# A gated cross-attention block: queries' features turned by VectorE in blocks and SBUF copies, and a reordered cycle

## The chip, the cores and the metric

The kernel runs on one core of a Trainium2 chip. The metric is the device time of one execution in microseconds (us), lower is better; several runs are taken and their median counts. A profile of one execution records every instruction of the five engines: TensorE (PE, matrix products, with its weight loads as PEld), VectorE (DVE), ScalarE (ACT), GpSimd (POOL) and SyncE (SP), which here only issues DMA transfers. Each engine works through its own queue in order; engines wait for one another by semaphores.

## The reference

For each of 32 samples, `x` has 256 tokens of 256 features, and the context has 77 rows of 256. All is float32. Two residual blocks follow one another.

The first is cross attention without a softmax. Tokens and context rows are normalized and projected by the same `w_in` to 8 heads of 128 features (`f_q`, `f_k`; values are the keys' features too):

```
cosine = f_q . f_k / (|f_q| |f_k|)
q_ratio = 2 min(var(f_q), 1) / (var(f_q) + 1)        (k_ratio likewise)
mixed  = cw * cosine + vw * cosine * decorr + ww * q_ratio * k_ratio
x      = x + tanh(g_xattn) * ((mixed @ f_v) @ w_out.T + b_out)
```

The weights `cw, vw, ww` and `decorr` are one number per head, from means and the correlation of all queries' features over all samples. The second block is self attention with 16 heads of 16 and a softmax over 256 keys, then two products each followed by a length normalization, and a GELU:

```
z = softmax(q k / 16) v;  z = norm(z @ Wo);  z = norm(z @ Wff)
x = x + tanh(g_ffn) * gelu(z)
```

## The kernel before, in words

A first part of about 140 us loads weights and inputs, forms the sums over all samples and the per-head weights, and brings samples 0 and 1 on their way. Then one loop (its body is the list `cycle`, L1157) runs over cycle numbers `n`. An entry `(ahead, stage, ...)` runs that stage for sample `n + ahead`, so in one cycle self attention of sample `n`, cross attention of `n + 1`, query and key features of `n + 2`, inputs of `n + 3` and the last products of `n - 1` are interleaved. The list is the order: the wrapper `InOrder` (L22) keeps the instructions of PE, ACT, DVE and POOL in program order. Almost all instructions therefore carry the line of the wrapper, L30, and are told apart by their tiles. DMAs from SP (`nc.sync`) aren't wrapped: their place in SP's queue is chosen by the framework when the kernel is built.

A sample's stages that matter here:

- `norm_inputs`, `transpose_inputs` (L194, L205): normalized tokens `xn`, turned by PE and scaled into `xTc`.
- `query_features(b, t, hh)` (L371): per half of the tokens `t` and of the heads `hh`, two products of 128x512 into PSUM, copied to `fq` by ACT (`hh` 0) or DVE (`hh` 1). `fq` is a tile of 128 tokens x 1024 features.
- `scale_queries(b, t)` (L388): DVE statistics of the 8 heads (`qst`, `qt`), POOL's power for 1/length (`rq`), POOL's product that scales `fq` in place, and the ratio into the padded tile `qrps[t]`.
- `transpose_queries(b, t, hh)` (L403): PE turns four 128x128 blocks of `fq` by a product with the identity `ident` into a PSUM tile; ACT or DVE copies it to `fqT`. Four calls a sample: 16 transposes, two ACT copies, two DVE copies.
- `key_features` (L224) forms context features in tiles `fvx` of 128 rows over sample borders; `measure_keys` (L242) takes their statistics in the cycles in which a tile is complete; `align_keys` (L252) copies a sample's 77 rows by DMA to `fv` and `nr`; `weigh_keys`, `scale_keys` (DVE writes the scaled selection `dk`) and `transpose_keys` (PE, `fvT`) follow, then `key_outputs` (`vw`, keys times `w_out`).
- `query_ratios`, `query_scores(b, pair)` (L341, L352): scores of the queries `fqT` and keys `fvT` into `s`; `attend` (L417): `s` times `vw` added to `x`.
- Self attention: `ff_stats`, `ff_norm` (`xf`), `ff_transpose`, `ff_project`, `ff_values`; then four units `u`, each with `scores` (PE to two PSUM tiles `sc`, DVE's maxima `nm`), `exponents` (ACT, with sums), `scale_values` (DVE, `vz`, values over sums) and `mix_values` (PE, `zp`). A unit with the stages listed after its scores is called a cluster. `ff_out` to `ff_gelu` finish sample `n - 1`, `ff_add` adds and stores it.

PSUM tiles for everything but scores and mixes (`mm_tile`) are three, used in turn; a product waits until the copy out of its tile's last user is done. `fqT`, `s`, `xTc`, `xf` have one buffer, `fq` and `fv` two, `x` eight. The x load of a later sample waits for the store of the sample that held its buffer.

Of the kernel before, what the change touches and what calls it, by code (L numbers as in the profile page):

```python
# [8 lines left out]
F32 = mybir.dt.float32  # L9
AF = mybir.ActivationFunctionType  # L10
ALU = mybir.AluOpType
# [3 lines left out]
P = 128  # L15
H = 8
# [17 lines left out]
def gated_block_kernel(  # L34
# [102 lines left out]
    def mm_tile():  # L137
        return ps.tile([P, 512], F32, tag="mm", name="mm")
# [54 lines left out]

    def norm_inputs(b):  # L194

        xn = pa.tile([P, NT, D], F32, tag="xn", name="xn", bufs=1)
        for t in range(NT):
            i = b * NT + t
            pool.tensor_scalar(
                xn[:, t, :], kept[b]["x"][:, t, :], mv_x[:, i, 0:1], rstd_x[:, i : i + 1],  # L200
                ALU.subtract, ALU.mult,
            )
        kept[b]["xn"] = xn
# [106 lines left out]
    def paired(pt, k, pair, rhs):  # L310

        for c in range(2):
            for i in range(2):
                h = 4 * pair + 2 * c + i
                pe.matmul(
                    pt[MA * i : MA * (i + 1), c * S : (c + 1) * S],
                    lhsT=k["fvT"][:, h, 0:MA], rhs=rhs[:, h, :], start=True, stop=True,
                )

    def key_outputs(b, pair):  # L320


        k = kept[b]
        if "vw" not in k:
            k["vw"] = pa.tile([P, 5, D], F32, tag="vw", name="vw", bufs=2)
        pg = mm_tile()
        if pair < 2:
            paired(pg, k, pair, woutT)
# [12 lines left out]
    def query_ratios(b):  # L341

        k = kept[b]
        k["s"] = pa.tile([P, 5, S], F32, tag="s", name="s", bufs=1)
        k["pr"] = mm_tile()
        for t in range(NT):
            pe.matmul(
                k["pr"][:, t * P : (t + 1) * P], lhsT=qrps[t].rearrange("p h w -> p (h w)"),
                rhs=ident, start=(t == 0), stop=False,
            )  # L350

    def query_scores(b, pair):  # L352

        k = kept[b]
        if pair < 2:
            pg = mm_tile()
            paired(pg, k, pair, k["fqT"])
            out = k["s"][:, 2 * pair : 2 * pair + 2, :].rearrange("p g q -> p (g q)")
            (act.copy if pair == 0 else dve.tensor_copy)(out, pg)
            return  # L360
        pg = k.pop("pr")
        for i in range(2):
            for j in range(4):
                n = MR + 16 * i
                pe.matmul(
                    pg[32 * j : 32 * j + n, 0:S], lhsT=k["fvT"][:, 2 * j + i, MA : MA + n],
                    rhs=k["fqT"][:, 2 * j + i, :], start=False, stop=(i == 1),
                )
        act.copy(k["s"][:, 4, :], pg[:, 0:S])

# [17 lines left out]
    def scale_queries(b, t):  # L388

        k = kept[b]  # L390
        fq = k["fq", t]
        m2, n2, rt = head_stats(lambda h: fq[:, h * P : (h + 1) * P], P, H, "q")
        rq = pa.tile([P, H], F32, tag="rq", name="rq")
        rsqrt_of(rq, n2)
        fq_h = fq.rearrange("p (h d) -> p h d", d=P)
        pool.tensor_tensor(
            fq_h, fq_h, rq.unsqueeze(2).to_broadcast([P, H, P]), ALU.mult
        )
        dve.scalar_tensor_tensor(
            qrps[t][:, :, MR], m2, P - 1.0, rt, ALU.min, ALU.mult  # L400
        )

    def transpose_queries(b, t, hh):  # L403
        k = kept[b]
        if (t, hh) == (0, 0):
            k["fqT"] = pa.tile([P, H, S], F32, tag="fqT", name="fqT", bufs=1)
        pt = mm_tile()
        for i in range(4):
            h = hh * 4 + i
            pe.transpose(  # L410
                pt[:, i * P : (i + 1) * P], k["fq", t][:, h * P : (h + 1) * P], ident
            )
        out = k["fqT"][:, hh * 4 : hh * 4 + 4, t * P : (t + 1) * P]
        src = pt.rearrange("p (h q) -> p h q", q=P)
        (dve.tensor_copy if hh else act.copy)(out, src)

    def attend(b, t):  # L417

# [215 lines left out]
    def load_w_out():  # L634
        nc.sync.dma_start(out=w_out_n, in_=w_out.rearrange("(c p) e -> p c e", p=P))

    wf_n = sw.tile([P, 2, D], F32, name="wf_n")

    def load_ff(*pairs):
        for w_t, w in pairs:  # L640
# [159 lines left out]
        act.copy(w1T.rearrange("p c o -> p (c o)"), pt[:, 0 : 2 * P])  # L800
        act.copy(w2T, pt[:, 2 * P : 2 * P + 3])

    woT = sw.tile([P, 2, D], F32, name="woT")

    def transpose_wo():
        pt = mm_tile()
# [52 lines left out]
    par16 = const.tile([P, 2], F32, name="par16")  # L859
    qrps, vzs = [], []  # L860
    for i in range(2):
        qrps.append(const.tile([P, H, 16], F32, name=f"qrp{i}"))
        vzs.append(const.tile([P, 4, 4, 16], F32, name=f"vz{i}"))
    eyes = const.tile([M, 2, SL], F32, name="eyes")
    offd = sw.tile([P, P], F32, name="offd")
# [3 lines left out]
    def set_constants():  # L869
        dve.memset(sel, 0.0)  # L870
        dve.memset(sel[:, MR + 1 : MR + 2], 1.0)


        pool.memset(par[:, 0:1], 0.0)
        pool.memset(par[:, 1:2], 1.0)
        for j in range(4):
            pool.memset(par[32 * j : 32 * j + 16, 0:1], 1.0)
            pool.memset(par[32 * j : 32 * j + 16, 1:2], 0.0)
        pool.tensor_scalar(par16, par, 1.0 / 16.0, None, ALU.mult)
        for qrp in qrps:  # L880
# [12 lines left out]
        dve.tensor_scalar(offd, ident, -1.0, 1.0, ALU.mult, ALU.add)  # L893
# [64 lines left out]
    for c in range(2):  # L958
        pe.transpose(pt[0:2, c * P : (c + 1) * P], lb[:, c, :], ident)
        pe.transpose(pt[0:2, D + c * P : D + (c + 1) * P], bl[:, c, :], ident)  # L960
    lbT = sw.tile([2, 2 * D], F32, name="lbT")
    dve.tensor_copy(lbT, pt[0:2, :])

    gs = sw.tile([P, 2, D], F32, name="gs")
# [144 lines left out]
    run(0, transpose_queries, 0, 0)  # L1109
    run(0, transpose_queries, 0, 1)  # L1110
    pt = mm_tile()
    pe.matmul(
        pt[:, 0 : 2 * H], lhsT=ones[0:H, :], rhs=dg.rearrange("p w h -> p (w h)"),
# [11 lines left out]
    for pair in (2, 0, 1):  # L1125
        run(0, key_outputs, pair)
    run(1, key_features)
    run(0, transpose_queries, 1, 0)
    run(0, transpose_queries, 1, 1)
    run(0, query_ratios)  # L1130
    for pair in range(3):
        run(0, query_scores, pair)
# [25 lines left out]
        (4, load_queries),  # L1158
        (-1, mix_values, 3),
        (0, scores, 0),  # L1160
        (2, transpose_inputs),
        (0, exponents, 0, 0),
        (-1, ff_out, 0),
        (-1, ff_out, 1),
        (0, exponents, 0, 1),
        (1, transpose_queries, 1, 0),
        (1, transpose_queries, 1, 1),
        (2, query_features, 0, 0),
        (1, query_ratios),
# [48 lines left out]
        (1, ff_project, "q"),  # L1218
# [42 lines left out]
```

## Time and profile before

| what | value |
|---|---|
| median of 3 runs (lowest, highest) | 1499.01 us (1497.58, 1503.09) |
| profiled execution, its own time | 1491.96 us |
| its span, first to last instruction | 1490.2 us |
| PE busy | 1439.0 us, 97% |
| DVE, ACT, POOL busy | 1078.1, 938.0, 531.1 us |
| mean granted TensorE clock | 0.983 |

"Busy" is the time in which an engine works on at least one instruction; products overlap inside PE, so the mean duration of one (273 ns for a transpose) is more than its share of the busy time (66.8 us for 512). A float32 product is recorded as two instructions, a transpose as one. The slices cut the span in 40 equal parts of 37 us and give each engine's busy share in tenths. The chain that ended last follows the waits back from the last instruction. A group line gives line, engine, operation, tiles written and read, shapes and count, then busy us and mean ns, then idle time of the engine ahead of it and what ended it. A window line gives start:end, length, each engine's busy us with counts in the order PE, PEld, DVE, ACT, POOL, then the granted clock, the DMA engines' share and GB/s. A timeline line gives start and duration in us, then the instruction, and in brackets the engine's idle time ahead of it and what ended it; several alike are merged.

### The profile page before, as it was taken

The numbers are of one execution on the slowest core, as the hardware profiler recorded it, in microseconds if no ns is written. First come the engines' busy times: TensorE is split into PE (matmuls) and PEld (weight loads), VectorE is DVE, ScalarE is ACT, GpSimd is POOL, SyncE is SP. The second block draws the span as 40 slices with busy tenths as digits, with TensorE's granted clock in tenths as the row PEclk, the third lists the DMA queues.
The fourth block names the chain that finished last, engine by engine and source line by source line (L and its number), as shares of the span: only waits on it lengthen the run. The fifth ranks groups of instructions, "written<-read, shape, count | busy, mean of one in ns | idle before, by whom it ended". The sixth has DMA issues, their size and how long they took to land.

```text
span 1490.2 us, 26481 instructions
## 1 busy us (share of the span) xinstructions
PE 1439.0 (97%) x9313; PEld 863.3 (58%) x9313; DVE 1078.1 (72%) x3053; ACT 938.0 (63%) x3038; POOL 531.1 (36%) x656
## 2 busy tenths in 40 slices
PE   6898999999999999999999999999999999999985
PEld 5754556666555555666655555665655555655641
DVE  5735678777777777787776777787777768787853
ACT  5621557666667666666667666666666756666675
POOL 5912233433243233333333333333333334333310
PEclk9989999999999999999999999999999999999996
DMA  8500000000000000000000000000000000000000
GB/s 267 169 15 27 9 10 24 21 26 13 21 24 15 24 24 18 29 24 14 19 18 22 24 24 21 27 17 23 17 20 24 19 24 16 18 14 12 8 8 14
DMA packets 26194, 43.31 MB, mean 29 GB/s; under 512 B 6010, under 2 KB 11055, under 8 KB 26062
## 3 DMA queue, kind: packets, MB, share of 16 engines
q1 hardware_dynamic: 25230, 41.63, 8.8%
q8 instruction: 73, 1.20, 0.3%
q14 instruction: 59, 0.48, 0.1%
q10 hardware_dynamic: 832, 0.00, 0.0%
HBM read 22.98 MB, written 8.39 MB: 21 GB/s over the span
## 4 chain that ended last, share of the span: by engine, by line
PE 88%; ACT 3%; DVE 3%; issue 1%; POOL 0%; ACTq 0%; POOLq 0%
PE mm L30 70%; PE sc L30 9%; PE zp L30 8%; ACT e L30 2%; ACT ge L30 1%; DVE u L30 1%; DVE nm L30 1%; ACT L30 0%; DVE kst L30 0%; DVE kt L30 0%; POOL i L30 0%; DVE vz L30 0%; POOL nrx L30 0%; DVE xTc L30 0%; ACT u L30 0%
## 5 line engine op out<-in xcount | busy, mean ns | idle before, releaser
L30 ACT ACTIVATE e<-sc,nm 128x256 f32<-128x256 f32 x1024 | 474.2, 491 | 143.9 <-DVE nm L30 143.9
L30 DVE TENSOR_REDUCE nm<-sc 128x4 f32<-128x1024 f32 x256 | 301.0, 1216 | 115.8 <-PE sc L30 115.8
L30 PE MATMUL mm<-winT,xTc 128*128 128x512 f32 x512 | 243.8, 608 | 6.4 <-DVE xTc L30 2.2
L30 ACT ACTIVATION_READ_ACCUMULATOR e<-sc,nm 128x1 f32 x1024 | 227.8, 222 | 0.0
L30 POOL TENSOR_TENSOR rq<-qt,nhalf 128x8 f32<-128x8 f32 x64 | 105.8, 1654 | 257.1 <-DVE qt L30 257.1
L30 PE MATMUL sc<-q,kTf 32*128 32x512 f32 x1024 | 153.1, 644 | 4.8 <-ACT e L30 4.8
L30 PEld LDWEIGHTS mm<-winT,xTc 128*128 128x128 f32 x512 | 92.2, 190 | 104.3 <-issue 71.4
L30 PE MATMUL mm<-vw,s 128*128 128x256 f32 x640 | 146.9, 384 | 0.0
L30 PE MATMUL zp<-e,vz 128*32 128x256 f32 x2048 | 138.9, 389 | 5.8 <-DVE vz L30 5.8
L30 POOL TENSOR_TENSOR fq<-fq,rq 128x1024 f32<-128x1024 f32 x64 | 135.0, 2109 | 5.0
L30 PEld LDWEIGHTS mm<-vw,s 128*128 128x128 f32 x640 | 119.0, 190 | 28.5 <-issue 13.7
L30 PE MATMUL mm<-w_of,zT 128*128 128x512 f32 x256 | 117.9, 604 | 0.8 <-DVE zT L30 0.8
L30 PEld LDWEIGHTS zp<-e,vz 128*32 128x32 f32 x2048 | 57.4, 110 | 95.5 <-issue 33.3
L30 POOL TENSOR_SCALAR i<-nn 128x2 f32<-128x2 f32 x64 | 14.2, 222 | 274.3 <-ACT ge L30 274.3
L30 ACT COPY vw<-mm 128x512 f32<-128x512 f32 x32 | 18.8, 586 | 145.1 <-PE mm L30 145.1
L30 DVE BATCH_NORM_STATS2 qst<-fq 128x6 f32<-128x128 f32 x512 | 103.9, 276 | 0.0
L30 PE MATMUL mm<-woutT,fvT 128*64 128x256 f32 (+2 forms) x1024 | 100.8, 384 | 0.1
L30 POOL TENSOR_SCALAR rs<-mv 128x1 f32<-128x1 f32 x64 | 15.8, 247 | 237.0 <-DVE mv L30 235.6
L30 PE MATMUL mm<-fqT,fvT 128*64 128x256 f32 (+2 forms) x1024 | 93.9, 383 | 0.0
L30 DVE TENSOR_TENSOR vz<-v,sums 128x128 f32<-128x128 f32 x128 | 86.8, 678 | 4.4
L30 ACT ACT_TABLE_LOAD x64 | 82.1, 1283 | 4.9 <-DMA x<-in_x_dram 4.1
L30 POOL TENSOR_SCALAR xn<-x,mv_x,rstd_x 128x256 f32<-128x256 f32 x64 | 79.1, 1248 | 10.3 <-issue 10.3
(203 smaller groups left out, 2401.3 us busy)
## 6 DMA issues: line engine op xcount, KB each, us to landing
x<-in_x_dram SPq DMA_DIRECT2D x64, 256.0 KB
out_dram<-x SPq DMA_DIRECT2D x32, 256.0 KB
fv<-fvx SPq DMA_DIRECT2D x13, 308.0 KB
ct<-in_ctx_dram SPq DMA_DIRECT2D x4, 512.0 KB
w_in_n<-in_L_xattn_w_in_dram SPq DMA_DIRECT2D x2, 512.0 KB
w_out_n<-in_L_xattn_w_out_dram SPq DMA_DIRECT2D x1, 1024.0 KB
ct<-in_ctx_dram SPq DMA_DIRECT2D x1, 384.0 KB
fv<-fvx SPq DMA_DIRECT2D x1, 304.0 KB
```

The lines of the kernel that those rows point to most:

```text
L30: return lambda *args, **kw: self._tc.keep_in_program_order(method(*args, **kw))
```

## The change

The 16 transposes on PE and the four copies out of PSUM of a sample are replaced, for samples 2 to 31, by `turn_queries`: per token half DVE transposes all 32x32 blocks of `fq` in one instruction into a tile `fb` with its blocks regrouped, and 16 DMAs of 32 partitions x 1 KB (32 rows `i` of blocks by column blocks `j`) carry the block groups across partitions into `fqT`. `fqT` now has the layout 128 x 8 token groups x 8 heads x 32 tokens, so a head's operand for the query scores is 8 runs of 32 columns. Samples 0 and 1 still use PE and the two copies.

The list `cycle` is reordered: query scores move from the second unit's cluster to the third, behind the third scores; all query features come in the first two clusters; `scale_keys`, the first `scale_queries` and `transpose_keys` come behind the query scores, `attend` behind them; `transpose_inputs` and `key_features` move to the end of the cycle. The two `ff_norm` follow the fourth scores. The second token half is turned early in the next cycle, behind the first scores; the first half behind the key outputs. The padded ratio tiles are doubled (`qrps[b % 2][t]`), and to fit, `xn`, `woT` and `lbT` share SBUF with tiles of the first part.

```diff
     def norm_inputs(b):
-        xn = pa.tile([P, NT, D], F32, tag="xn", name="xn", bufs=1)
+        xn = sw.tile([P, NT, D], F32, tag="wf_n", name="xn")
...
-            paired(pg, k, pair, k["fqT"])
+            paired(pg, k, pair, lambda h: k["fqT"][:, :, h, :])
...
-    def transpose_queries(b, t, hh):
-        k = kept[b]
-        if (t, hh) == (0, 0):
-            k["fqT"] = pa.tile([P, H, S], F32, tag="fqT", name="fqT", bufs=1)
-        pt = mm_tile()
+    def turn_queries(b, t):
+
+        k = kept[b]
+        if t == 0:
+            k["fqT"] = pa.tile([P, S // 32, H, 32], F32, tag="fqT", name="fqT", bufs=1)
+        if b < 2:
+            for hh in range(2):
+                pt = mm_tile()
...
+            return
+        fb = pa.tile([P, 4, H, 32], F32, tag="fb", name="fb", bufs=2)
+        dve.transpose(
+            fb.rearrange("p j h a -> p h j a"),
+            k["fq", t].rearrange("p (h j a) -> p h j a", j=4, a=32),
+        )
         for i in range(4):
-            h = hh * 4 + i
-            pe.transpose(
-                pt[:, i * P : (i + 1) * P], k["fq", t][:, h * P : (h + 1) * P], ident
-            )
-        out = k["fqT"][:, hh * 4 : hh * 4 + 4, t * P : (t + 1) * P]
-        src = pt.rearrange("p (h q) -> p h q", q=P)
-        (dve.tensor_copy if hh else act.copy)(out, src)
+            for j in range(4):
+                nc.sync.dma_start(
+                    out=k["fqT"][32 * j : 32 * j + 32, 4 * t + i],
+                    in_=fb[32 * i : 32 * i + 32, j],
+                )
...
-    woT = sw.tile([P, 2, D], F32, name="woT")
+    woT = sw.tile([P, 2, D], F32, tag="gs", name="woT")
...
-        qrps.append(const.tile([P, H, 16], F32, name=f"qrp{i}"))
+        qrps.append([const.tile([P, H, 16], F32, name=f"qrp{i}{t}") for t in range(NT)])
...
-    lbT = sw.tile([2, 2 * D], F32, name="lbT")
+    lbT = sw.tile([P, 2 * D], F32, tag="fc", name="lbT", bufs=2)[0:2]
...
         (0, scores, 0),
-        (2, transpose_inputs),
         (0, exponents, 0, 0),
+        (1, turn_queries, 1),
         (-1, ff_out, 0),
         (-1, ff_out, 1),
         (0, exponents, 0, 1),
-        (1, transpose_queries, 1, 0),
-        (1, transpose_queries, 1, 1),
         (2, query_features, 0, 0),
-        (1, query_ratios),
         (0, scale_values, 0),
+        (2, query_features, 0, 1),
         (-1, ff_norm_first),
         (-1, ff_norm_second),
         (0, scores, 1),
-        (1, query_scores, 0),
         (0, exponents, 1, 0),
-        (1, query_scores, 1),
-        (1, query_scores, 2),
         (0, exponents, 1, 1),
         (0, mix_values, 0),
         (2, measure_keys),
         (2, align_keys),
-        (2, query_features, 0, 1),
+        (3, norm_inputs),
+        (2, query_features, 1, 0),
         (0, scale_values, 1),
-        (3, key_features),
         (2, weigh_keys),
+        (2, query_features, 1, 1),
+        (1, query_ratios),
         (0, scores, 2),
+        (1, query_scores, 0),
+        (1, query_scores, 1),
         (0, exponents, 2, 0),
+        (1, query_scores, 2),
         (0, mix_values, 1),
+        (0, exponents, 2, 1),
         (2, scale_keys),
+        (2, scale_queries, 0),
+        (2, transpose_keys, 0),
+        (2, transpose_keys, 1),
         (1, attend, 0),
+        (0, scale_values, 2),
         (1, ff_stats, 0),
-        (2, scale_queries, 0),
         (1, attend, 1),
-        (0, exponents, 2, 1),
         (-1, ff_gelu),
         (2, warm_exponentials),
+        (1, ff_stats, 1),
+        (0, scores, 3),
         (1, ff_norm, 0),
-        (1, ff_stats, 1),
-        (0, scale_values, 2),
-        (2, query_features, 1, 0),
-        (2, query_features, 1, 1),
         (1, ff_norm, 1),
-        (3, norm_inputs),
-        (2, transpose_keys, 0),
-        (2, transpose_keys, 1),
-        (0, scores, 3),
         (0, mix_values, 2),
         (2, key_outputs, 2),
         (2, key_outputs, 0),
         (2, key_outputs, 1),
+        (2, turn_queries, 0),
+        (2, scale_queries, 1),
         (1, ff_transpose),
-        (2, transpose_queries, 0, 0),
+        (3, transpose_inputs),
         (0, exponents, 3, 0),
-        (2, transpose_queries, 0, 1),
-        (2, scale_queries, 1),
+        (3, key_features),
         (1, ff_project, "k"),
```

More of the change, by code (lines that the diff above doesn't have):

```diff
@@ L316, in paired @@
                     pt[MA * i : MA * (i + 1), c * S : (c + 1) * S],
-                    lhsT=k["fvT"][:, h, 0:MA], rhs=rhs[:, h, :], start=True, stop=True,
+                    lhsT=k["fvT"][:, h, 0:MA], rhs=rhs(h), start=True, stop=True,
                 )
@@ L327, in key_outputs @@
         if pair < 2:
-            paired(pg, k, pair, woutT)
+            paired(pg, k, pair, lambda h: woutT[:, h, :])
             out = k["vw"][:, 2 * pair : 2 * pair + 2, :].rearrange("p g c -> p (g c)")
@@ L347, in query_ratios @@
             pe.matmul(
[L348 removed]
+                k["pr"][:, t * P : (t + 1) * P], lhsT=qrps[b % 2][t].rearrange("p h w -> p (h w)"),
                 rhs=ident, start=(t == 0), stop=False,
@@ L366, in query_scores @@
                     pg[32 * j : 32 * j + n, 0:S], lhsT=k["fvT"][:, 2 * j + i, MA : MA + n],
-                    rhs=k["fqT"][:, 2 * j + i, :], start=False, stop=(i == 1),
+                    rhs=k["fqT"][:, :, 2 * j + i, :], start=False, stop=(i == 1),
                 )
@@ L399, in scale_queries @@
         dve.scalar_tensor_tensor(
-            qrps[t][:, :, MR], m2, P - 1.0, rt, ALU.min, ALU.mult
+            qrps[b % 2][t][:, :, MR], m2, P - 1.0, rt, ALU.min, ALU.mult
         )
-    def transpose_queries(b, t, hh):
+    def turn_queries(b, t):
         k = kept[b]
-        if (t, hh) == (0, 0):
-            k["fqT"] = pa.tile([P, H, S], F32, tag="fqT", name="fqT", bufs=1)
-        pt = mm_tile()
-        for i in range(4):
-            h = hh * 4 + i
-            pe.transpose(
-                pt[:, i * P : (i + 1) * P], k["fq", t][:, h * P : (h + 1) * P], ident
-            )
-        out = k["fqT"][:, hh * 4 : hh * 4 + 4, t * P : (t + 1) * P]
-        src = pt.rearrange("p (h q) -> p h q", q=P)
-        (dve.tensor_copy if hh else act.copy)(out, src)
+        if t == 0:
[3 more added lines that the diff above has]
+                pt = mm_tile()
+                for i in range(4):
+                    h = hh * 4 + i
+                    pe.transpose(
+                        pt[:, i * P : (i + 1) * P], k["fq", t][:, h * P : (h + 1) * P], ident
+                    )
+                (act.copy if hh == 0 else dve.tensor_copy)(
+                    k["fqT"][:, 4 * t : 4 * t + 4, hh * 4 : hh * 4 + 4, :],
+                    pt.rearrange("p (h i a) -> p i h a", h=4, a=32),
+                )
[4 more added lines that the diff above has]
+            k["fq", t].rearrange("p (h j a) -> p h j a", j=4, a=32),
+        )
+        for i in range(4):
+            for j in range(4):
+                nc.sync.dma_start(
+                    out=k["fqT"][32 * j : 32 * j + 32, 4 * t + i],
+                    in_=fb[32 * i : 32 * i + 32, j],
+                )
     def attend(b, t):
@@ L635, in load_w_out @@
         nc.sync.dma_start(out=w_out_n, in_=w_out.rearrange("(c p) e -> p c e", p=P))
-    wf_n = sw.tile([P, 2, D], F32, name="wf_n")
+    wf_n = sw.tile([P, 2, D], F32, tag="wf_n", name="wf_n")
     def load_ff(*pairs):
@@ L879, in set_constants @@
         pool.tensor_scalar(par16, par, 1.0 / 16.0, None, ALU.mult)
-        for qrp in qrps:
+        for qrp in qrps[0] + qrps[1]:
             pool.memset(qrp, 0.0)
@@ L960, in gated_block_kernel @@
         pe.transpose(pt[0:2, D + c * P : D + (c + 1) * P], bl[:, c, :], ident)
-    lbT = sw.tile([2, 2 * D], F32, name="lbT")
+    lbT = sw.tile([P, 2 * D], F32, tag="fc", name="lbT", bufs=2)[0:2]
     dve.tensor_copy(lbT, pt[0:2, :])
-    gs = sw.tile([P, 2, D], F32, name="gs")
+    gs = sw.tile([P, 2, D], F32, tag="gs", name="gs")
     for c in range(2):
@@ L1108, in gated_block_kernel @@
     dve.tensor_scalar(dg[:, 1, :], ident[0:H, 0:H], lg[:, 2:3], 4.0, ALU.mult, ALU.mult)
-    run(0, transpose_queries, 0, 0)
-    run(0, transpose_queries, 0, 1)
+    run(0, turn_queries, 0)
     pt = mm_tile()
@@ L1127, in gated_block_kernel @@
     run(1, key_features)
-    run(0, transpose_queries, 1, 0)
-    run(0, transpose_queries, 1, 1)
+    run(0, turn_queries, 1)
     run(0, query_ratios)
```

## The prediction

> **What bounds the kernel now.** I read the page first: busy times, the slices, the chain that ended last.
>
> ```profile
> PE 1439.0 (97%) x9313; PEld 863.3 (58%) x9313; DVE 1078.1 (72%) x3053; ACT 938.0 (63%) x3038; POOL 531.1 (36%) x656
> ...
> PE   6898999999999999999999999999999999999985
> ...
> PE 88%; ACT 3%; DVE 3%; issue 1%; POOL 0%; ACTq 0%; POOLq 0%
> ```
>
> TensorE (PE) is busy in all slices but the first three and the last two, and 88% of the chain is PE. Then one stretch of the steady state, a little over one sample long:
>
> ```profile
> 743.00:786.00 43.00, 42.85 (x284) 25.87 (x283) 34.01 (x104) 29.07 (x99) 16.31 (x18) 1.00 0.05 15
> ```
>
> PE idles 0.15 us in 43; VectorE (DVE, 34.0) and ScalarE (ACT, 29.1) have slack, and the clock is full. From output store to output store a cycle is 41.5 us (704.63, 746.13, 787.63), or 43.2 us where two key halves fall into it (787.63 to 830.84), about one in five: mean 41.84. So each us that PE gains or loses per cycle counts about 28 times.
>
> **What goes.** The timeline shows the two groups of eight transposes and what starts behind them:
>
> ```profile
> 710.17 1.04 PE L30 MATMUL mm<-ident,fq 128*128 128x128 f32 x8
> ...
> 711.36 1.98 PE L30 MATMUL mm<-winT,xTc 128*128 128x512 f32 x4 [0.15 <-DVE u L30]
> ...
> 739.46 1.04 PE L30 MATMUL mm<-ident,fq 128*128 128x128 f32 x8
> ...
> 740.33 1.96 PE L30 MATMUL mm<-xT,w_k 128*128 128x256 f32 x8
> ```
>
> Start to start: 1.19 + 0.87 = 2.06 us of PE per sample, for 30 of the 32 (samples 0 and 1 keep their transposes). Were all else hidden, 30 x 2.06 = 62 us would go. ACT also loses two copies (0.59 each) and DVE two (0.69).
>
> **What comes.** Per token half one DVE block transpose of 128x1024, T, and 16 SBUF-to-SBUF copies of 32 partitions x 1 KB on SyncE's queue (SP). The trace of before has neither.
>
> T: the Trainium skill, "VectorE: DVE Perf Modes", The three transpose paths, says that this transpose turns separate 32x32 blocks (hence the copies) and gives 311 ns for 128 columns of 2 bytes. At one column per 0.96 GHz cycle, 896 more make 1.24 us; the maximum over 1024 columns takes 1.22 here. I take 1.2. If 4-byte data went two per cycle it would be 0.65, at half rate 2.3.
>
> Copy issue: the last sample's keys, 77 rows from row 31 x 77 = 2387 = 18 x 128 + 83, end in a piece of 32 rows, so two SBUF-to-SBUF copies of 32 partitions are there:
>
> ```profile
> 1350.77 0.57 SPq L262 DMA_DIRECT2D fv<-fvx  x1
> ...
> 1391.38 0.53 SPq L263 DMA_DIRECT2D nr<-nrx  x1
> ```
>
> Back-to-back issues stand 0.05 apart (the page's key copies run 0.52 to 0.95 by row count). I take 0.60 a copy, 9.6 us for 16; ends 0.55 and 0.75. Landing: the x load waits for the store (704.63 to 706.67, 2.04 us); the skill, "DMA: Bandwidth & Descriptors", Anatomy of one DMA, puts about 2 us of fixed cost mostly into completion (for GpSimd's queue; here SP's agrees). A key row copy took 1.87 (763.53 to its reader at 765.40): I take 1.9.
>
> The bytes, 1 MB a sample, cost nothing while the DMA share is 0.05. The query scores' operand, now in runs of 32 columns, I cost at nothing; 0 to 0.3 us a cycle.
>
> **The new cycle walked.** PE by start-to-start times of the timeline: four scores 4.28, four value mixes 4.0, output products 3.43, query features 6.88, ratios 0.55, query scores 2.75, a key half 1.8, attend 4.42, key transposes 1.86, key outputs 3.09, two input transposes 0.99, three projections 5.32: 39.4; with the 2.06, 41.4, as measured. Zero is the first scores' start; new order without waits: second scores 8.0, third 14.0, query scores 15.1, key transposes 18.8.
>
> (a) Scaled keys `dk`. DVE's order behind the third scores is two maxima, the copy of `s`, then `dk`: 14.0 + 1.17 + 2.36 + 0.72 + 1.22 = 19.5, with the hand-over 19.6, against 18.8: 0.8 us late. Before, `dk` had 5 us of slack (726.8 against 732.07). With `measure_keys` in the cycle (three in five), its 3.1 us now follow the second maxima: 9.15 + 2.36 + 3.1 + 0.53 (values) + 0.70 (features' copy) = 15.85, when the third maxima could begin at 15.2. Another 0.65. Mean 1.2 us of PE waiting.
>
> (b) The second half's copies. First half: turned behind the key outputs' copies, at about 34.1; 16 issues run to 43.8, 2.3 into the next cycle (period 41.5). SP is in order: the store (held until then, 0.4), the x load, which waits 2.04 for it and issues to about 4.85, key copies inside that wait. The second half, turned at 4.75, follows: last issue 4.85 + 15 x 0.60 = 13.85, landed 15.75, query scores about 15.85 against 15.1: 0.75 late. Most of it lies within (a), since the copy of `s` has 0.35 to 1.0 us of room: 0.15 net. Behind the query scores on PE stands all of the cycle's rest, and ACT's and DVE's copies of `s`, the third exponents behind them, wait with it. (After eight copies in flight each waits for the eighth before it, which 8 x 0.60 = 4.8 us ago has landed.) This step is steep, 31 issues long: at 0.55 an issue nothing is late, at 0.65 two us, at 0.70 three to four.
>
> (c), (d) DVE's scaled values `vz`. One in four of these took 1.94 instead of 0.29:
>
> ```profile
> 732.10 1.90 POOL L30 TENSOR_TENSOR fq<-fq,rq 128x1024 f32<-128x1024 f32 x1
> ...
> 732.20 1.94 DVE L30 TENSOR_TENSOR vz<-v,sums 128x128 f32<-128x128 f32 x1
> ...
> 745.15 0.29 DVE L30 TENSOR_TENSOR vz<-v,sums 128x128 f32<-128x128 f32 x1
> ...
> 745.50 2.36 POOL L30 TENSOR_TENSOR fq<-fq,rq 128x1024 f32<-128x1024 f32 x1
> ```
>
> The skill, "SBUF — State Buffer", Who interferes with whom: a VectorE instruction with two SBUF inputs and a GpSimd instruction that reads SBUF exclude each other; the first holds the ports to its end. Both pairs agree. New places: `dk` ends about 20.5, statistics 2.6, `rq` 1.65, so GpSimd scales from 24.75 to 26.9, and the third `vz` (attend's first half and the x update are done at 25.3) stops until then. That delays the second update, its statistics, two maxima, `xf` and the first key output copy, which frees the PSUM tile of the `xf` transposes: about 32.3 against 31.9, 0.45 (c). The other scaling comes T later in DVE's queue than before: 38.4 to 40.5, and the fourth `vz`, behind the last exponents (39.3), falls into it; before it was 0.35 us ahead. The fourth mix waits 0.45 (d).
>
> Each of three or four restarts shows part of a weight load (0.11 to 0.19): 0.35.
>
> Sum: 1.2 + 0.15 + 0.45 + 0.45 + 0.35 = 2.6 against 2.06: 0.5 us slower per cycle, 28 x 0.5 = 14 us; in the last cycles, without query features, the 9.6 us of issue have less cover (2), which the extra two turned samples' gain cancels. Span 1490.2 + 14 = 1504, its execution 1491.96 + 14 = 1506. The median of the runs is 7.05 above that execution: 1499.0 + 14 = 1513.
>
> Hidden: T's own 2.4 us less 1.4 of copies (DVE has 9 us idle a cycle; it counts only through (c), (d)); the moved key features, whose copies feed SP half a cycle before `measure_keys`; two more `qrp` tiles (0.5 us of start-up memsets); tiles shared with `wf_n`, `gs`, `fc`, all dead before their next use.
>
> **Rivals.** (1) Faster: the waits stay smaller than the gain. If `vz` isn't caught (scaling shifts 1 us against either), (c), (d) and their restarts fall away: 2.6 - 1.1 = 1.5, gain 0.55 x 28 = 15; with a quicker T or issues also (b): 0.75 x 28 = 21: 1478 to 1484. It decides where the stalls sum to under 1.8 a cycle (7.5 us over 28). For: PE at 97% and the 62 us are sure. Against: (a) rests on rows of the trace alone. (2) SP becomes the bound: over 0.62 an issue, 32 copies, a store's landing and a load no longer fit between turning and use. 0.65: 0.8 more a cycle, 1535; 0.70: 2.1 more, 1572. For: other piece sizes took to 0.95. Against: both 32-row issues were under 0.58. (3) T at 2.3: 1.6 more a cycle, 1558. (4) A wash, stalls equal to the gain, 1492 to 1506.
>
> **Chances.** My forecast (1507 to 1526) 0.36, rival 1 0.22, 2 0.17, 3 0.07, wash 0.18. A measurement tells 0.5% from no change (7.5 us: 1491.5 and 1506.5): faster 0.22, same 0.18, slower 0.60. Range 1480 to 1555: it leaves out the far ends of 1 and 2, about 0.1 each. Cases of both signs hold most of it, so mine alone: 1507 to 1526.
>
> **What would show it.** Right: PE idle before the key transposes on `dk` (0.8 to 1.5 a cycle) and before query scores on DMA (up to 1); `vz` at about 2 us twice a cycle; SP issues of 0.55 in rows of 16; PE busy near 92 to 94%. Wrong: PE waits under 1.8 a cycle in all (faster); SP issuing without pause and query scores waiting 2 us or more (rival 2); T over 2 us (rival 3). The `s` copies or exponents in place of `dk` would mean that I misplaced the queue ahead of it.

## The result and the profile after

The changed kernel takes 1581.66 us, median of 4 runs (1578.7 to 1584.25), against 1498.3 (1497.04 to 1503.09) for the kernel before on the same chip: ratio 1.055, 95% interval 1.052 to 1.058. I had predicted 1513 with a range of 1480 to 1555. The direction was right, the loss is 83 us instead of 14.

The page of the changed kernel, its busy times, slices and chain:

```profile
PE 1422.1 (90%) x8833; PEld 827.4 (52%) x8833; DVE 1096.6 (70%) x3053; ACT 906.2 (57%) x2978; POOL 515.4 (33%) x660
...
PE   6898999999989999899989799999999897999986
...
PE 50%; SPq 17%; DMA 8%; ACT 8%; DVE 7%; issue 4%; POOL 1%; DVEq 0%; ACTq 0%; POOLq 0%
PE mm L30 40%; SPq L428 16%; ACT e L30 6%; PE zp L30 5%; PE sc L30 5%; DMA x<-in_x_dram 3%; DMA fqT<-fb 3%; DVE nm L30 2%; DVE vz L30 1%; DMA fv<-fvx 1%; DVE dk L30 1%; ACT ge L30 1%; ACT kTf L30 1%; DMA out_dram<-x 1%; DMA nr<-nrx 1%
```

TensorE does 480 products less and is only 17 us less busy; it now idles for 10% of the span. In the chain PE has fallen from 88% to 50%, and the largest piece that stands there instead is SP's queue with one line, L428: the issues of the copies. A window of the same length as before has the loss in one line:

```profile
700.00:743.00 43.00, 39.79 (x259) 22.99 (x258) 32.73 (x93) 25.39 (x85) 14.51 (x16) 0.96 0.18 48
```

PE idles 3.2 us of 43 instead of 0.15, and the granted clock is 0.96 instead of 1.00. PE's timeline shows where:

```profile
708.39 1.13 PE L30 MATMUL sc<-q,kTf 32*128 32x512 f32 x6
712.47 4.56 PE L30 MATMUL mm<-fqT,fvT 128*64 128x256 f32 x32 [2.95 <-DMA nr<-nrx]
716.86 1.04 PE L30 MATMUL zp<-e,vz 128*32 128x256 f32 x16
717.83 2.02 PE L30 MATMUL mm<-dk,fv 77*128 77x96 f32 x16
```

Nearly all the idle time stands before the query scores (0.26 us more before the last value mixes), and these take 4.39 us from start to next start. In the kernel before it was 2.75, without a wait:

```profile
714.79 2.93 PE L30 MATMUL mm<-fqT,fvT 128*64 128x256 f32 x32
717.54 1.05 PE L30 MATMUL zp<-e,vz 128*32 128x256 f32 x16
```

In the changed kernel the key transposes (`dk`) follow without a wait. The releaser printed, `nr`, is inferred and not to be trusted here; SP's timeline of the same stretch tells what was late:

```profile
689.88 8.02 SPq L428 DMA_DIRECT2D fqT<-fb  x11
698.01 0.53 SPq L626 DMA_DIRECT2D out_dram<-x  x1
698.64 1.67 SPq L262 DMA_DIRECT2D fv<-fvx  x2
700.41 0.43 SPq L188 DMA_DIRECT2D x<-in_x_dram  x1
700.94 10.15 SPq L428 DMA_DIRECT2D fqT<-fb  x16
```

SP issues without a pause from the first half's row through the store, the key rows and the x load to the end of the second half's row at 711.1. The last issue began at 710.5 and PE starts at 712.47: the 1.97 us of a landing (from a DMA's issue to the moment when its reader may start). This is a cycle with key rows between the two rows of copies. In 11 other cycles it is the x load that holds the queue, 1.5 us on average, until the store before it has landed. Two lines of SP's waits (total us, times, longest) between 250 and 1450 us:

```profile
SPq L428 <- DMA fv<-fvx: 30.1, 9, 10.1
SPq L188 <- DMA out_dram<-x: 16.4, 11, 1.8
```

The first of them returns below. A group view of the turn, duration as minimum, median and maximum in ns:

```profile
L428 SPq DMA_DIRECT2D fqT<-fb x960: 507/589/1884, 199.1 to 1509.1; - x192
L30 DVE STREAM_TRANSPOSE fb<-fq x60: 1229/1235/1246, 197.7 to 1497.3; 128x1024 f32<-128x1024 f32 x60
```

VectorE's turn is 1.235 us, as taken. A copy's issue is 0.589, plus 0.045 to the next: 0.634 in a row (16 in 10.15 us).

For a balance I took PE's records between the 5th and the 27th store (22 cycles): each block's time from its start to the next block's start without idle, plus the idle time ahead of it, per cycle in us.

| block of PE | before | after | after, keys split | order alone, late turn | through HBM, keys split |
|---|---|---|---|---|---|
| query transposes | 1.92 | - | - | 2.09 + 0.07 | - |
| query features | 7.08 + 0.14 | 7.06 | 7.06 | 7.17 | 7.06 |
| query scores | 2.75 | 4.02 + 3.70 | 3.56 + 2.27 | 2.75 | 2.75 |
| key transposes | 1.85 | 1.85 + 0.03 | 1.84 + 0.06 | 1.83 + 0.45 | 1.85 + 0.49 |
| value mixes | 3.87 | 3.92 + 0.20 | 3.94 + 0.20 | 3.94 | 3.94 + 0.19 |
| cycle | 41.82 | 45.05 | 43.17 | 42.46 | 40.43 |

After against before: 2.06 us of transposes gone as predicted, 3.70 of waiting and 1.27 of slower running added at the query scores, 0.23 at other waits, and about 0.1 elsewhere: 3.23 a cycle. 28 cycles make 90; the two profiled executions differ by 86.7 us, the medians by 83.

Two things in this were new to me. First, the waits are not alike: most are 1 to 3 us, but six are 4.9 to 11.1. The longest, in SP's timeline:

```profile
875.75 1.63 SPq L262 DMA_DIRECT2D fv<-fvx  x2
877.49 0.92 SPq L188 DMA_DIRECT2D x<-in_x_dram  x1
878.83 19.19 SPq L428 DMA_DIRECT2D fqT<-fb  x16
```

The DMA traffic of the same stretch, 876 to 902 us in 40 slices of 0.65 us:

```profile
GB/s 309 151 176 107 98 239 134 71 79 69 73 79 28 25 25 25 25 32 25 25 25 25 25 25 24 8 51 51 51 51 55 52 54 54 54 35 5 5 2 0
```

Within the row no copy is issued from 882.5 to 891.8, while something moves at 25 GB/s. That is a piece of key rows: 55 and 73 rows were issued at 875.75 and 876.70, and the seventh copy, the eighth issue behind the 73 rows, waits for their landing (the first line of SP's waits above). The Trainium skill, "DMA: Bandwidth & Descriptors", Why a DMA increments its semaphore by 16 and not by 1, says that a DMA is spread over the largest number of engines up to 16 that divides its slowest dimension; 73 is prime, so one engine should move the 292 KB; the 25 GB/s of the trace agree (at this rate they take 12.0 us, and the queue goes on 15.1 us after their issue). The six long waits fall into the cycles with pieces of 53, 74, 29, 73, 31 and 71 rows: five primes, and 74, which is 2 x 37. (Pieces of 23 and 47 rows were issued half a cycle ahead of the row, and the waits were 2.3 and 1.9 us.)

Second, the clock. A window behind a wait of 2.02 us at 396.0 to 398.0:

```profile
398.94:402.36 3.42, 3.42 (x26) 1.50 (x26) 1.50 (x2) 2.42 (x9) 0.00 (x0) 0.50 0.02 5
```

PE is busy all the 3.42 us, at half the clock. Between 250 and 1400 us the granted clock falls to 0.5 in 19 such stretches: 13 of 3.41 us, each at a wait of 2.0 to 3.3 us, and six of 6.83 or 13.65 us around the six long waits. Three more waits of 2.1 to 2.7 us and all four below 2 us have none, and the kernel before has none in its full cycles. The Trainium skill, "TensorE: Matmul & The Clock Gate", Part 1: The HAM clock gate (the "warmup" mystery), describes a free-running window of 3413 ns and half the clock after one idle window. The length agrees; but here waits of 2 to 3 us, shorter than a window, were enough, in most cycles and not in all.

The records show which. All 38 ends of the 19 stretches lie on one grid of 3.413 us, to within 3 ns, so the windows are fixed in time and don't start with a wait. I cut PE's records by this grid: the windows at full clock that a halved one follows have 1.86 to 3.41 us of idle PE (19 windows); of the 288 that a full one follows, one has 1.93 and the others at most 1.65. So a wait of 2 to 3 us halves the clock where about 1.9 us of it lie in one window, and not where a border splits it more evenly. (In the other runs the limit is less sharp: a few windows with 1.0 to 1.9 us of idle time fall on either side.)

### The profile page after: what moved, and what is told of

It reads as the page before. It is cut to its first block, busy times and chain, and to the rows that moved or that the text cites. A ratio compares the mean times of both kernels' runs of the same rounds, so it can differ in the third digit from the quotient of the medians.

```text
span 1576.9 us, 26858 instructions
## 1 busy us (share of the span) xinstructions
PE 1422.1 (90%) x8833; PEld 827.4 (52%) x8833; DVE 1096.6 (70%) x3053; ACT 906.2 (57%) x2978; POOL 515.4 (33%) x660
## 4 chain that ended last, share of the span: by engine, by line
PE 50%; SPq 17%; DMA 8%; ACT 8%; DVE 7%; issue 4%; POOL 1%; DVEq 0%; ACTq 0%; POOLq 0%
PE mm L30 40%; SPq L428 16%; ACT e L30 6%; PE zp L30 5%; PE sc L30 5%; DMA x<-in_x_dram 3%; DMA fqT<-fb 3%; DVE nm L30 2%; DVE vz L30 1%; DMA fv<-fvx 1%; DVE dk L30 1%; ACT ge L30 1%; ACT kTf L30 1%; DMA out_dram<-x 1%; DMA nr<-nrx 1%
## 5 line engine op out<-in xcount | busy, mean ns | idle before, releaser
L30 PE MATMUL mm<-winT,xTc 128*128 128x512 f32 x512 | 237.7, 606 | 1.2 <-ACT fqT L30 1.0
L30 ACT ACTIVATION_READ_ACCUMULATOR e<-sc,nm 128x1 f32 x1024 | 219.0, 214 | 0.0
L30 PE MATMUL mm<-fqT,fvT 128*64 128x256 f32 (+2 forms) x1024 | 128.5, 480 | 98.7 <-DMA fqT<-fb 41.7
L30 PE MATMUL sc<-q,kTf 32*128 32x512 f32 x1024 | 158.2, 653 | 3.5 <-ACT e L30 3.5
L30 PEld LDWEIGHTS mm<-fqT,fvT 128*64 128x64 f32 (+2 forms) x1024 | 64.3, 144 | 171.2 <-issue 158.1
L30 ACT COPY s<-mm 128x512 f32<-128x512 f32 x64 | 30.8, 482 | 183.3 <-PE mm L30 183.1
L30 DVE RECIPROCAL sums<-sums 128x8 f32<-128x8 f32 x128 | 25.5, 199 | 143.8 <-ACT e L30 143.8
L30 POOL TENSOR_TENSOR fq<-fq,rq 128x1024 f32<-128x1024 f32 x64 | 121.4, 1896 | 5.0
L30 DVE COPY s<-mm 128x512 f32<-128x512 f32 x32 | 22.1, 691 | 115.3 <-PE mm L30 115.3
L30 PE MATMUL mm<-woutT,fvT 128*64 128x256 f32 (+2 forms) x1024 | 94.2, 382 | 0.7 <-DVE fvT L30 0.7
```

The lines of the kernel that those rows point to most:

```text
L30: return lambda *args, **kw: self._tc.keep_in_program_order(method(*args, **kw))
```

## The experiments

Theory A, formed on the trace: SP's 32 in-order issues don't fit between a sample's turning and its use, so the query scores wait, and each wait costs clock on top. Rival B: the reordered cycle (late `dk`, `vz` held by GpSimd) or the strided operand costs the time. Rival C: not the issues but the landing of the copies is late.

**The order alone.** All samples turned by PE, the rest as changed:

```diff
-        if b < 2:
+        if True:
             for hh in range(2):
```

> The changed kernel with all 32 samples' queries turned by PE (the two copies out of PSUM included) at the places where the changed kernel turns them; order of the cycle, layout of fqT and its strided operand stay. Nothing is turned by VectorE and no copy is issued. Theory A (SP's 32 copies of 0.635 us are what is too long): the wait before the query scores is gone, the reorder costs little: 1500 to 1530 us. Rival B (the reordered cycle itself, by dk, xf and vz, or the strided operand, costs the time): 1560 us or more, with PE waiting on dk, vz or xf as before.

Measured 1551.65 us (1547.33 to 1556.54), ratio 1.036 (1.033 to 1.040): neither. Its timeline has a wait that belongs to neither theory:

```profile
736.25 0.60 ACT L30 COPY fqT<-mm 128x512 f32<-128x512 f32 x1
...
736.90 1.98 PE L30 MATMUL mm<-w_of,zT 128*128 128x512 f32 x4 [1.07 <-ACT fqT L30]
```

The changed order calls the second turn behind the first exponents; with PE turning, ACT's copy out of PSUM then stands behind four exponents, and the last products wait for its tile. The experiment itself had made a wait. The query scores ran 2.75 us with the new layout's operand, so the strided operand is excluded. The same with the turn where the kernel before has it:

```diff
         (0, exponents, 0, 0),
-        (1, turn_queries, 1),
         (-1, ff_out, 0),
         (-1, ff_out, 1),
         (0, exponents, 0, 1),
+        (1, turn_queries, 1),
```

> The run with the order alone (all queries turned by PE), with the second half's turn moved behind the last products' and the second exponents' places, where the kernel before has it. In that run PE waited 1.3 us a cycle inside the last products for ScalarE's copy of fqT, which stood behind four exponents. If this is what the order alone cost, 1552 - 1.2 x 28 = 1510 to 1525 remain (a late dk, 0.46 a cycle, and small ones). If the reorder costs by itself (rival B): 1545 or more.

1518.98 us (1518.04 to 1521.95), ratio 1.016 (1.014 to 1.017), in the expected band. So the order costs about 22 us with PE turning, and rival B is out as the main cause. Most of what is left is PE's wait before the key transposes, 0.45 us a cycle:

```profile
698.27 2.00 PE L30 MATMUL mm<-dk,fv 77*128 77x96 f32 x16 [0.52 <-ACT s L30]
```

**The turn alone**, in the order of before (query scores in the second cluster). The part of its difference from the kernel before that lies in the list `cycle`:

```diff
         (0, exponents, 0, 0),
+        (1, turn_queries, 1),
         (-1, ff_out, 0),
         (-1, ff_out, 1),
         (0, exponents, 0, 1),
-        (1, transpose_queries, 1, 0),
-        (1, transpose_queries, 1, 1),
...
-        (2, transpose_queries, 0, 0),
+        (2, turn_queries, 0),
         (0, exponents, 3, 0),
-        (2, transpose_queries, 0, 1),
```

> The kernel before with its order of the cycle, and only the turning replaced: VectorE's block transpose and 16 copies on SP per token half, the second half turned behind the first exponents, the first half behind the input transposes (shared SBUF as in the changed kernel). Query scores stay in the second unit's cluster, some 9 us into a cycle instead of 15. Theory A (SP's row of issues is too long): the copies end at about 17.6 us, so PE waits 8 to 9 us a cycle, less the 2.06 saved, more for the halved clock behind the wait: 1690 to 1750. Rival B (the reorder is what costs): 1440 to 1500.

1841.81 us (1835.65 to 1847.45), ratio 1.231 (1.228 to 1.234). PE's waits of 250 to 1450 us:

```profile
PE mm L30 <- DMA fqT<-fb: 237.4, 23, 13.0
PE mm L30 <- ACT xT L30: 15.5, 23, 0.7
```

A wait of 10.3 us a cycle, and 4.78 us for the scores at the reduced clock: both longer than expected, the mechanism as in A. Without the reorder the turning would have cost four times as much; the reorder is what makes most of the copies fit.

**Two queues.** Half of the second half's copies issued on ScalarE's queue:

```diff
-                nc.sync.dma_start(
+                (nc.scalar if t == 1 and i % 2 else nc.sync).dma_start(
```

> The changed kernel with 8 of the 16 copies of the second token half (every second row of blocks i) issued on ScalarE's DMA queue instead of SP's. Bytes, sizes, landing and order of the cycle are the same; only SP's second row is 8 x 0.635 = 5.1 us shorter. Theory A: the 2 to 3 us wait before the query scores and the halved clock behind it go: 1582 - 28 x (2.6 + 1.1) = 1480, or up to 1515 where the late dk (1.2 a cycle), until now hidden in that wait, comes out. Rival B: PE waits elsewhere, 1560 or more. Rival C (not the issue but the landing of the copies is late): 1575 to 1585.

1743.65 us (1742.51 to 1746.18), ratio 1.165 (1.162 to 1.168): none of the three. PE's and ACT's timelines:

```profile
779.44 0.69 PE L30 MATMUL sc<-q,kTf 32*128 32x512 f32 x4
780.06 2.93 PE L30 MATMUL mm<-fqT,fvT 128*64 128x256 f32 x32
...
815.90 3.78 PE L30 MATMUL mm<-winT,xTc 128*128 128x512 f32 x4 [4.64 <-DVE u L30]
```

```profile
809.49 5.38 ACTq L428 DMA_DIRECT2D fqT<-fb  x8
814.91 0.38 ACT L30 ACTIVATE ge<-mm 128x256 f32<-128x256 f32 x1 [5.71 <-DMA fqT<-fb]
```

The wait before the query scores is gone and they run at full clock. This doesn't yet exclude C: PE now waits 7.5 us a cycle ahead of the query scores and comes to them 22 to 36 us after a cycle's first scores (15.5 in the changed kernel, without the wait), so that a late landing would be hidden too. ACT's instructions stand in order behind its own issues, 0.67 us each; it idles 5.7 us before the `ge` that frees a PSUM tile, and PE waits there instead (the view names `u`, which shares the tile). I had not asked what is queued behind the issues on ACT.

**Fewer issues, on SP.** Two runs. First the key rows: pieces without a divisor from 4 to 16 are issued as a multiple of 16 rows and a rest.

```diff
-            nc.sync.dma_start(out=k["fv"][at : at + n], in_=fvx[i % 4][row : row + n])
+            wide = n // 16 * 16 if n > 16 and not any(n % d == 0 for d in range(4, 17)) else n
+            for a, m in ((0, wide), (wide, n - wide)):
+                if m:
+                    nc.sync.dma_start(
+                        out=k["fv"][at + a : at + a + m], in_=fvx[i % 4][row + a : row + a + m]
+                    )
```

> The changed kernel with each copy of key rows (fv) whose row count has no divisor from 4 to 16 (73, 71, 53, 74, 31, 29, 47, 57, 46 rows) issued as two, of 16, 32, 48 or 64 rows and the rest. If the six waits of 4.9 to 11.1 us come from such a copy (the trace has the 73 rows move at 25 GB/s for 12 us, and the seventh copy of the second half wait for its end), they shrink to the usual 2 to 3 us: 1582 - 27 = 1550 to 1560, with no wait over 4 us left. If they have another cause: 1580 to 1585.

1544.75 us (1531.3 to 1549.82), ratio 1.034 (1.032 to 1.036): 37 us less than the changed kernel, a little more than expected, and no wait over 3.6 us is left. (The profiled execution is the fastest of them, so the table flatters this run.) On top of it, 28 copies a sample instead of 32. The last two blocks of each token half are left out, so that these parts of `fqT` keep an earlier sample's values; for this `fqT` is one tile for all samples:

```diff
+    fqT = const.tile([P, S // 32, H, 32], F32, name="fqT")
...
-            k["fqT"] = pa.tile([P, S // 32, H, 32], F32, tag="fqT", name="fqT", bufs=1)
+            k["fqT"] = fqT
...
-            for j in range(4):
+            for j in range(4 if i < 3 else 2):
```

> The run with the key rows split (1545 us, PE waits 2.3 us a cycle before the query scores), with 28 copies a sample instead of 32: the last two blocks of each token half (i = 3, j = 2 and 3) are left out from sample 2 on, so those parts of fqT keep an old sample's values; fqT is one tile made once. Theory A (the number of issues in a row is what makes the query scores wait): SP is done 4 x 0.635 = 2.5 us earlier, the wait falls to about 0.2 and the halved clock with it, dk's 0.44 comes out: 1545 - 28 x (2.1 + 0.8 - 0.4) = 1475 to 1490. If the wait is set by something that does not grow with the number of issues (the landing, VectorE's turn, the key rows): 1535 to 1545.

1466.43 us (1463.45 to 1470.74), ratio 0.979 (0.977 to 0.981), below the expected band. Four issues, 2.5 us of SP's time, are worth 78 us, 2.8 a cycle. PE's waits are now mostly those for `dk`, `e` and `vz`, with little of the copies:

```profile
PE mm L30 <- DVE dk L30: 11.2, 20, 1.6
PE sc L30 <- ACT e L30: 7.2, 7, 1.5
PE mm L30 <- DMA fqT<-fb: 6.1, 6, 1.9
PE zp L30 <- DVE vz L30: 5.1, 20, 0.3
```

This is the run that decides for A: same engine, same order, each copy of the same size and with the same landing of about 2.1 us where a wait is left; only the rows are shorter. It also speaks against C, since a landing that is late by itself would have stayed late.

**The clock by itself.** Work that nobody needs, in the place where PE waits:

```diff
+        if pair == 0 and b >= 2:
+            dry = mm_tile()
+            for i in range(16):
+                pe.transpose(dry[:, i % 4 * P : (i % 4 + 1) * P], ident, ident)
```

> The changed kernel with 16 products of 128x128 (identity by identity, written to a PSUM tile that nobody reads; some 2.0 us of PE) ahead of each sample's query scores from sample 2 on. They add work that is thrown away, in the place where PE waits for the copies. If the halved clock after the wait is a cost of its own (about 1.6 us in some 17 cycles): 1582 - 27 + 3 = about 1558. If the wait alone counts and the clock does not: 1580 to 1590, up by what the filling is longer than the wait.

1567.03 us (1562.71 to 1568.56), ratio 1.046 (1.043 to 1.049): 15 us faster than the changed kernel with 1.96 us of products more in each cycle.

```profile
699.81 1.97 PE L30 MATMUL mm<-ident 128*128 128x128 f32 x16
702.58 2.93 PE L30 MATMUL mm<-fqT,fvT 128*64 128x256 f32 x32 [0.80 <-DMA nr<-nrx]
```

Time at half clock falls from 4.03 to 1.71 us a cycle, and the query scores run 3.27 us instead of 4.02. So the halved clock is a cost of its own; the gain is less than my 24, and the clock that is left low fits the long waits, which 2 us don't fill.

**Through HBM.** Two landings, five DMAs a half: out with 128 partitions x 4 KB, back with four of 32 partitions x 4 KB:

```diff
+    dr = ctx.enter_context(tc.tile_pool(name="dr", bufs=2, space=bass.MemoryType.DRAM))
...
-        for i in range(4):
-            for j in range(4):
-                nc.sync.dma_start(
-                    out=k["fqT"][32 * j : 32 * j + 32, 4 * t + i],
-                    in_=fb[32 * i : 32 * i + 32, j],
-                )
+        hb = dr.tile([P, 4, H * 32], F32, tag="hb", name="hb")
+        nc.sync.dma_start(out=hb, in_=fb.rearrange("p j h a -> p j (h a)"))
+        for j in range(4):
+            nc.sync.dma_start(
+                out=k["fqT"][32 * j : 32 * j + 32, 4 * t : 4 * t + 4].rearrange("p i h a -> p i (h a)"),
+                in_=hb[:, j].rearrange("(i p) f -> p i f", p=32),
+            )
```

> The changed kernel with the block groups of fb brought across the partitions through HBM: per token half one DMA of 128 partitions x 4 KB out to a scratch tensor and four DMAs back into fqT (32 partitions x 4 pieces of 1 KB each). 10 issues a sample instead of 32, but two landings in a row (about 4 us) and twice the bytes. Theory A: the copies are in time, PE's transposes are saved: 1440 (all 2.06 us a sample gained) to 1505 (with dk, xf and vz as predicted, 2.4 us a cycle). Rival B: 1550 or more. Rival C: two landings take longer than one, so the wait before the query scores grows: 1600 or more.

1473.69 us (1470.93 to 1477.69), ratio 0.984 (0.981 to 0.986), in the band of A and faster than both kernels. With two landings in a row, C would have made it slower. SP's timeline of one half:

```profile
702.20 0.32 SPq L428 DMA_DIRECT2D hb<-fb  x1
704.85 1.74 SPq L430 DMA_DIRECT2D fqT<-hb  x4
```

4.4 us from the first issue to the end of the last, the landing between them included, where the 16 copies took 10.15. Then with the split key rows, and with `dk` ahead of VectorE's copy of the scores:

```diff
         (0, scores, 2),
+        (2, scale_keys),
...
-        (2, scale_keys),
```

> The changed kernel with three edits: the turn through HBM (5 DMAs a half), the key rows split as in the run on them, and the scaled keys (dk) made right behind the third maxima, ahead of VectorE's copy of the scores. Of the run through HBM (cycle 40.99 us) PE's waits for dk (0.44 a cycle) and before the query scores (0.41) should go: 1474 - 0.85 x 28 = 1450 to 1460. If neither wait was the bound: 1470 to 1477.

1463.77 us (1459.3 to 1468.46), ratio 0.979 (0.976 to 0.981), a little short. VectorE's and PE's timelines:

```profile
716.82 1.79 DVE L30 TENSOR_TENSOR vz<-v,sums 128x128 f32<-128x128 f32 x1
...
723.02 0.42 DVE L30 TENSOR_TENSOR vw<-mm,bias_t 128x256 f32<-128x256 f32 x1
...
723.49 0.66 PE L30 MATMUL mm<-ident,xf 128*128 128x128 f32 x4 [0.37 <-DVE vw L30]
```

PE still waits 0.38 before the key transposes (for a PSUM tile, ACT's copy of `s`), and a new 0.50 before the transposes of `xf`: the third `vz` is now held 1.79 us by GpSimd, and the tile comes late. The split rows without the earlier `dk`, and the exchange of two key outputs (`(2, key_outputs, 0)` ahead of `(2, key_outputs, 2)`) on top of all three edits:

> The turn through HBM and the split key rows, with the scaled keys (dk) where the changed kernel has them. Beside the run with all three edits (1463.8 us) this tells which of the two further edits brought the 10 us from 1473.7. If the key rows: 1462 to 1467, with the waits of up to 4.6 us before the query scores gone. If the earlier dk: 1472 to 1475.

> The run with all three edits, and the first two products of the key outputs exchanged, so that ScalarE's copy and not VectorE's frees the PSUM tile that the transposes of xf take. Those waited 0.50 us a cycle for VectorE's vw, which stood behind a vz held 1.8 us by GpSimd's scaling. If that tile is the wait: up to 0.4 x 28 = 11 us less, 1453 to 1458. If xf itself is as late as the tile: 1461 to 1466.

1456.89 us (1454.11 to 1461.03), ratio 0.974 (0.972 to 0.976), for the first, below its expected band; 1461.39 (1460.17 to 1464.01), 0.977 (0.975 to 0.978), for the second, in which the wait for `xf` is gone and as much has come back in small amounts at the key outputs, the value mixes and `attend`. So the split rows brought the gain, and the earlier `dk` cost some. The best kernel, turn through HBM and split rows, is faster than before by 2.6% (2.4 to 2.8). Busy times of its page, and two lines of PE's timeline:

```profile
PE 1386.4 (95%) x8833; PEld 811.7 (56%) x8833; DVE 1099.6 (76%) x3053; ACT 904.4 (62%) x2978; POOL 515.0 (35%) x660
```

```profile
703.56 2.93 PE L30 MATMUL mm<-fqT,fvT 128*64 128x256 f32 x32
...
707.75 2.00 PE L30 MATMUL mm<-dk,fv 77*128 77x96 f32 x16 [0.39 <-DVE dk L30]
```

SP is out of its chain of work that ended last, and the query scores wait for nothing.

## Why the prediction was wrong in size

The step that failed is (b), the second half's copies: 0.15 us net in the sum, 3.70 us of waiting and 1.27 of slower running on the chip. Three terms of it were mis-sized or missing. That the direction came out right was luck: in my sum 2.45 of the 2.6 us came from (a), (c), (d) and the restarts, and where the copies are in time (through HBM, keys split) only 0.68 us of waits is left and the kernel is faster than before.

- **The price of an issue.** I took 0.60 from two copies of 32 rows that stood alone (0.57 and 0.53 us). In a row it is 0.634, which makes 1.05 us over 31 issues; I had called the step steep and put two us at 0.65. The run with 28 copies comes to 32 at about 0.555 each: there little is late, which my "at 0.55 an issue nothing is late" said. On top come long issues, 1.0 to 1.9 us for 27 of the 960 copies, roughly one a sample; what makes these long was not found. With the key rows split, the wait is 2.27 us a cycle. In that run, as medians over samples 3 to 27 and counted like my walk from the first scores, the turn ends at 4.68 (I had 4.75) and the first row at 2.8 (2.3). The store, the keys and the load between the rows take 3.2 us and not 2.55, so the second row begins at 6.0 (4.85), and its last issue begins at 15.7 (13.85). Without a wait PE would come to the scores at 15.5 (15.1).
- **The wait for the eighth before, "which 8 x 0.60 = 4.8 us ago has landed".** True of copies, which land in 2 us. At the start of the second row, the eighth before can be a piece of key rows, and that of 73 rows held it 9.2 us. I had priced the key rows only by their issue. Splitting them took 37 us off; in the profiles, where the split run is at its fastest, 1.43 us of waiting a cycle.
- **The clock.** I costed a wait of PE at its length. Behind 19 of the 22 waits of 2 us or more (250 to 1400 us) the clock is halved for 3.4 us or more: 1.27 us a cycle at the query scores. I had not looked for it, since the kernel before has no such wait in its cycle.

The other steps, one by one. The saving of 2.06 us a sample came in full. T was right (1.235 for 1.2), the landing too (1.97 for 1.9), and the strided operand costs nothing. (a), `dk` late by 1.2, was not seen, because it lies within the longer wait of (b); uncovered, it is 0.40 to 0.49, and in about half of those cycles of the two HBM runs (in all of them where PE turns) PE waits for ACT's copy of `s` to free a tile and not for `dk`, which my last paragraph named as a misplaced queue. (c), the third `vz`, cost nothing in the changed kernel, where it took 1.12 us on average; it came as 0.50 a cycle where `dk` had been moved. The restarts (0.35) don't show: the cycle through HBM with split keys, 40.43 us, is the old 41.82 less 2.06 plus the 0.68 of waits. (d), the fourth `vz`, is 0.20 instead of 0.45:

```profile
735.13 1.90 POOL L30 TENSOR_TENSOR fq<-fq,rq 128x1024 f32<-128x1024 f32 x1
...
736.24 0.94 DVE L30 TENSOR_TENSOR vz<-v,sums 128x128 f32<-128x128 f32 x1
```

The overlap is there, but only the last 0.8 us of the scaling fall on it; my walk had 1.2 (from 39.3 to 40.5). Of the two pairs of lines on which I had based (c) and (d) only the first overlaps; in the second `vz` had ended before the scaling began, so it shows no holding.

Rival 2, SP as the bound, was the right mechanism, with the sign that I had named for it: SP without a pause, the query scores waiting 2 us or more. It fell short in time (1535 at 0.65; 1582 at 0.634), since it lacked the key rows, the clock and the long issues. Rival 1 is what the kernel through HBM shows: with the copies in time, the small waits of the order leave about 40 of the 62 us.

Still open: why some issues take two to three times the usual, and where exactly, between 1.0 and 1.9 us of idle time in a window, the clock falls.

## What to carry to other kernels

Price a row of DMA issues from a row, not from one that stands alone, and add up an in-order queue from the time when its data is made to the time when it is used: if everything queued between (stores, loads, other copies) nearly fills that time, a few per cent of an issue decide. Ask of every transfer in the queue how its rows divide, and what waits on its semaphore; and ask, before moving issues to a compute engine's queue, what stands behind them. A wait of TensorE that reaches 2 us can cost more than its length, so a step that is late by that much should be costed with the clock.

## What was unexpected of the hardware

- The issue's time did not grow with bytes: 128 partitions x 4 KB to HBM took 0.32 us on SP, 32 partitions x 4 KB back 0.44 each in a row, 32 partitions x 1 KB from SBUF to SBUF 0.63, the same from ScalarE's queue 0.67.
- A copy of 73 rows of 4 KB moved at 25 GB/s and held the queue 9.2 us; the rows split into 64 and 9 did not.
- TensorE's clock was halved for 3.41 us behind 13 of 16 waits of 2.0 to 3.3 us and behind none of four shorter ones. In the changed kernel it fell after each window of a fixed 3.41 us grid that held 1.95 us or more of idle TensorE, and after none with 1.65 or less; 2 us of products without a use, put there, made the kernel 15 us faster.
